# Tiles of B and C from the common ring of a selective scan, and a group of its output matmuls moved by one unit

## Chip, cores and metric

The kernel runs on one core of a Trainium2 chip, in one launch, on an input of 16 samples. The metric is the device time of that core in microseconds (us). The time before is the median of three runs. The profile is one further execution, recorded by the hardware profiler.

## What is computed

Each sample is an image of 256 channels and 32 x 32 positions, so L = 1024 tokens. Two layers are applied, each behind a group normalisation and with a residual sum: an attention layer with four heads and a feed-forward part, and a selective scan (Mamba) with 512 inner channels d and 64 states n. The scan is what matters here:

```
u     = silu(causal_conv(in_proj(x)))              # [L, 512]
dt, Bm, Cm = split(u @ x_proj_w.T, [16, 80])       # Bm, Cm: [L, 64]
delta = softplus(dt @ dt_proj_w.T + dt_proj_b)     # [L, 512]
A     = -exp(A_log)                                # [512, 64]
for t in range(L):
    h = exp(delta[t, :, None] * A) * h + (delta[t] * u[t])[:, None] * Bm[t, None, :]
    y[t] = sum over n of h[:, n] * Cm[t, n]
out   = ((y + u * D) * silu(z)) @ out_proj_w.T * gate
```

## The kernel before, in words

**Units and blocks.** The scan of a sample is cut into 256 units. A unit holds two channels: 64 states of each fill the 128 partitions, and time runs along 1024 columns. Eight units make a block, which fills one of two tiles h0 and h1 in turn (parity e, line 934). The main loop (L1014 to L1055) goes through all 4096 units of the 16 samples; `at` is the unit's place in its sample, i its place in its block.

**A unit's steps.** `load` (L895) fetches a row pair of delta u from DRAM, spread over 64 partitions each, into a tile dub (L913). `inputs` (L916) multiplies it by B on POOL (L918). `decay` (L920) makes delta on PE from three bf16 pieces, by two matmuls into PSUM (L927), and takes exp(delta A) on ACT (L929). `scan` (L931) is one DVE instruction (L935) from those two into h. In iteration n the program writes load(n+6), inputs(n+4), scan(n), decay(n+2), in this order. The exp's PSUM tile has two buffers, so decay(n+2) needs scan(n) to be done.

**Outputs.** `outputs` (L952) makes the sum over n with C, block by block, while the next block is scanned. It is a generator: each iteration of the main loop takes it to its next `yield`, ahead of the scan and of decay(n+2). A block has 16 groups (r, s) of matmuls (L960), which read all of its h tile and a spread form of C, cd. After the four groups of each r ACT copies 256 columns to y2 (L966). Before, a yield stands after every second group, so that in each of the eight units of the next block PE takes two groups. In the ninth unit 32 small matmuls turn the result (L972), ACT copies it to yo (L976), and three units later it is stored (L983). The h tile of a block is written again by the block after the next, whose first scan waits for the last group.

**B and C.** At a sample's first load (L898) the tiles bt and ct are fetched, each row of B and C to two partitions (L903). Before, they come from the pool hst with one buffer each. bt is read by every product of the sample. ct is read on ACT by `spread_c` (L941, L944) at units 7 and 8 of the sample, which fills cd, and by nothing afterwards. At a block's first load the pieces of delta are fetched too (L909). The tiles dub come from the pool dutp with seven buffers.

**Side work.** The next sample's attention and scan inputs (`prepare`, L985) and the previous one's gate and output (`gate_and_store`, L836) are generators as well, whose steps are dealt out between the units at a rate set from the steps' shares (L1029, L1052 to L1055). What remains is done at unit 250 (L1030), where the input of the sample after the next is fetched too.

**Queues.** PE, ACT, DVE and POOL keep the order in which the program is written: L1066 to L1076 chain their instructions. Every DMA is issued from SP. SP's order isn't in that chain; it is fixed when the kernel is built, and a DMA can stand ahead of its place in the program where its tile and its data are there (the last sample's ct is issued at 12036.8 us, its bt at 12147.5). When the kernel runs, SP is one queue in order: a DMA that waits for its tile holds what stands behind it. A pool's tiles with one tag share its buffers: a new tile takes the one that comes free.

## Time and profile before

| | |
|---|---|
| median of 3 runs | 12829.15 us (12777.23 to 12891.25) |
| profiled execution | 12813.5 us |
| its span | 12811.7 us |
| mean granted TensorE clock | 0.796 |
| DVE, POOL, PE, ACT busy | 88%, 78%, 77%, 61% of the span |
| first scan starts, last scan starts | 444.0 us, 12761.2 us |
| scans: number, mean | 4096, 2276 ns |
| products with B: number, mean | 4096, 2417 ns |
| exps: number, mean | 4096, 1090 ns |

The span runs from the first to the last instruction of the program, and the execution's time is taken around it. Times in the timeline count from the span's start. A group of the profile shows line, engine, operation, tiles written and read with their shapes and their number; then its busy time in us and the mean duration in ns; then the engine's idle time just before its instructions, with what ended it. In the list of an instruction's waits the two numbers are the total in us and how often. In the timeline the first number is the start, the second the length of a merged stretch, x the number of instructions in it, and the bracket the idle time before it with what ended it. SPq is SP's queue of DMAs; its busy time is that of issuing, and the data moves afterwards.

### The profile page before, as it was taken

Reading aid. Unit: us, or ns where it says so; the run is one execution under the profiler, and the core shown is the slowest. Engines: PE = TensorE matmul, PEld = TensorE weight load, DVE = VectorE, ACT = ScalarE, POOL = GpSimd, SP = SyncE. Lnnn points to the kernel's source line nnn. Section 1 sums busy time; section 2 is a strip of 40 time slices with the busy share of each in tenths; the row PEclk is TensorE's granted clock in tenths of the full one; section 3 lists DMA queues with packets and bytes.
Section 4 is the critical chain, followed back from the end, with each engine's and each line's share of the span. In section 5 each row is a group of like instructions: output and inputs, shape, how many; then the busy total and the mean of one; then the engine's idle time right before and its main releaser. Section 6 shows DMA issues by size and latency. Waiting matters only on the chain. (4 is left out here: it accounts for less than half of the span.)

```text
span 12811.7 us, 424772 instructions
## 1 busy us (share of the span) xinstructions
PE 9896.8 (77%) x186800; PEld 5493.9 (43%) x186800; DVE 11279.1 (88%) x7480; ACT 7776.4 (61%) x10933; POOL 10022.9 (78%) x4201
## 2 busy tenths in 40 slices
PE   6676977868778687886878778697786877868776
PEld 2344444444444444444444444444444444444444
DVE  2789898898988899898998988999888998989998
ACT  3566665656656566566666656666565665656654
POOL 0587877878788787887878778887787878878798
PEclk7887977879878797887878878797787978868756
DMA  1567666676676766767676676766767667676776
GB/s 49 170 218 236 222 219 223 220 242 214 219 234 219 241 213 218 235 215 243 212 233 230 217 237 212 244 218 215 231 219 240 218 218 237 216 240 211 230 251 229
DMA packets 1038405, 2820.13 MB, mean 220 GB/s; under 512 B 290370, under 2 KB 368451, under 8 KB 1036548
## 3 DMA queue, kind: packets, MB, share of 16 engines
q1 hardware_dynamic: 1036548, 2792.97, 66.0%
q8 instruction: 1459, 23.90, 0.8%
q14 instruction: 398, 3.26, 0.1%
HBM read 2513.82 MB, written 261.62 MB: 217 GB/s over the span
## 5 line engine op out<-in xcount | busy, mean ns | idle before, releaser
L918 POOL TENSOR_TENSOR dub<-dub,bt 128x1024 f32<-128x1024 f32 x4096 | 9797.2, 2417 | 2640.4 <-DMA dub<-dus 2468.9
L935 DVE TENSOR_TENSOR_SCAN h<-a,dub 128x1024 f32<-128x1024 f32 x4096 | 9205.6, 2276 | 799.1 <-ACT a L929 475.0
L929 ACT ACTIVATE a<-a,acol 128x1024 f32<-128x1024 f32 x4096 | 4463.7, 1090 | 2870.7 <-PE a L927 2749.6
L960 PEld LDWEIGHTS yb<-h,cd 128*32 128x32 f32 x131072 | 2503.1, 129 | 2812.0 <-issue 1278.9
L960 PE MATMUL yb<-h,cd 128*32 128x64 f32 x131072 | 3274.4, 253 | 479.5 <-ACT y L966 331.3
L927 PE MATMUL a<-pieces,pick 48*128 48x512 bf16 x8192 | 1910.4, 458 | 2158.6 <-DVE h L935 2047.7
L927 PEld LDWEIGHTS <-pick 48*128 48x128 bf16 x8192 | 569.6, 95 | 2564.1 <-issue 2156.1
L966 ACT COPY y<-yb 128x256 f32<-128x256 f32 x2048 | 762.2, 372 | 721.7 <-PE yb L960 713.4
L499 PE MATMUL av<-pt,vv 128*64 128x512 f32 x2048 | 611.0, 677 | 3.0 <-ACT sums L488 1.6
L519 ACT ACTIVATE pt<-st_ps 128x512 f32<-128x512 f32 x1024 | 552.9, 597 | 89.2 <-PE st_ps L511 88.2
L972 PE MATMUL yb<-turn,y 128*32 128x16 f32 x32768 | 592.1, 214 | 7.1 <-issue 5.9
L511 PE MATMUL st_ps<-sp 33*128 33x512 f32 x2048 | 591.3, 653 | 2.9 <-ACT pt L519 2.9
L972 PEld LDWEIGHTS yb<-turn,y 128*32 128x32 f32 x32768 | 574.1, 159 | 8.3 <-issue 6.8
L440 PE MATMUL s_ps<-kd,q 32*64 32x512 f32 x2044 | 543.5, 618 | 17.1 <-DVE mx L419 9.0
L440 PE MATMUL s_ps<-k,q 32*64 32x512 f32 x2048 | 518.4, 593 | 0.0
L976 ACT COPY yo<-yb 128x128 f32<-128x128 f32 x512 | 135.6, 265 | 598.2 <-PE yb L972 586.1
L696 PE MATMUL g_ps<-w,xp 128*128 128x256 f32 x1464 | 455.2, 450 | 0.0
L419 DVE CUSTOM_DVE_ANT_0 over<-s_ps,over 128x512 f32<-128x512 f32 x512 | 342.9, 671 | 82.3 <-ACT over L445 44.6
L696 PEld LDWEIGHTS g_ps<-w,xp 128*128 128x128 f32 x1464 | 368.1, 326 | 66.5 <-issue 58.8
L445 ACT ACTIVATE over<-s_ps 128x512 f32<-128x512 f32 x511 | 303.3, 594 | 40.0 <-PE s_ps L440 40.0
L872 PE MATMUL m_ps<-w,xs 128*128 128x256 f32 x1024 | 318.3, 461 | 11.5 <-POOL xs L847 11.5
L682 DVE SCALAR_TENSOR_TENSOR u<-up,cwh,u 128x1024 f32<-128x1024 f32 x192 | 281.4, 1466 | 28.0 <-ACT u L674 27.7
(182 smaller groups left out, 7363.9 us busy)
## 6 DMA issues: line engine op xcount, KB each, us to landing
dub<-dus SPq DMA_DIRECT2D x4096, 512.0 KB
dps<-pc SPq DMA_DIRECT2D x384, 128.0 KB
pieces<-dps SPq DMA_DIRECT2D x1024, 48.0 KB
xs<-in_x_dram SPq DMA_DIRECT2D x64, 512.0 KB
xs<-kept SPq DMA_DIRECT2D x64, 512.0 KB
zs<-z SPq DMA_DIRECT2D x64, 512.0 KB
ud<-u SPq DMA_DIRECT2D x64, 512.0 KB
dus<-du SPq DMA_DIRECT2D x64, 512.0 KB
```

Of the source, the lines that this page charges most:

```text
L440: nc.tensor.matmul(s[ts(e, 64)], q4[r, ts(c, 64)], keys[r], start=True, stop=True)
L499: nc.tensor.matmul(av[ts(e, 2 * DH)], vv[j // (NJ // 2)][:, j % (NJ // 2), 2 * pair + e, :], pts[e], start=(j == 0), stop=(j == NJ - 1),)
L511: nc.tensor.matmul(s, ka[r, ts(j, P)], qa[r, hs(hf)], start=True, stop=True)
L519: nc.scalar.activation(pt, s, AF.Exp)
L696: nc.tensor.matmul(ps[:, ts(q, C)], xp[k][:, ds(first + t, P, 4)], wg_s[:, k, t, :], start=(k == 0 and t == 0), stop=False,)
L918: nc.gpsimd.tensor_tensor(v, v, blocks[units[n][0]]["bt"], ALU.mult)
L927: nc.tensor.matmul(a[:, hs(hf)], w, pieces[r], start=True, stop=True)
L929: nc.scalar.activation(a, a, AF.Exp, scale=acol[:, at : at + 1])
L935: nc.vector.tensor_tensor_scan(now["h", e][:, i, :], decays.pop(n), loaded.pop(n), 0.0, ALU.mult, ALU.add)
L960: nc.tensor.matmul(yb[ts(g, 32), ts(s, 64)], cd[:, at // 16, ts(c, 32)], hbuf[:, :, at : at + 8], start=(c == 0), stop=(c == 1),)
L966: nc.scalar.copy(y2[:, r], yb[:, :256])
L972: nc.tensor.matmul(some[ts(r, 32), x], y2[:, r, x:256:8], turn[:, x], start=True, stop=True)
```

## The change

bt and ct now come from the pool dutp, under the tag of the dub tiles, and that pool has nine buffers instead of seven. The pool hst loses the two. The memory taken is the same: 7 + 2 tiles of 4 KB a partition before, nine after. A buffer that bt or ct leaves can be taken by a dub tile and the other way round.

In `outputs` the yield after group (3, 1) goes to after group (3, 2). The seventh unit so takes the groups (3, 0), (3, 1) and (3, 2), and the eighth takes (3, 3) and the copy to y2. The number of yields stays.

```diff
@@ -79,7 +79,7 @@
-    dutp = pool("dutp", 7)
+    dutp = pool("dutp", 9)
@@ -896,8 +896,8 @@
         if (k, q, e, i) == (0, 0, 0, 0):
-            bt = hst.tile([P, L], F32, name="bt", tag="bt")
-            ct = hst.tile([P, L], F32, name="ct", tag="ct")
+            bt = dutp.tile([P, L], F32, name="bt", tag="dub")
+            ct = dutp.tile([P, L], F32, name="ct", tag="dub")
             for v, lo in ((bt, 0), (ct, NS)):
                 src = st["rows"][lo : lo + NS, :]
                 nc.sync.dma_start(v, src.unsqueeze(1).to_broadcast([NS, 2, L]))
@@ -964,7 +964,7 @@
                 if s == 3:
                     nc.scalar.copy(y2[:, r], yb[:, :256])
-                if s % 2 == 1:
+                if s % 2 == 1 and (r, s) != (3, 1) or (r, s) == (3, 2):
                     yield
```

## The prediction

> **What bounds the kernel now.** I read the page first: which engine is full, and which rows fill it.

> ```profile
> span 12811.7 us, 424772 instructions
> PE 9896.8 (77%) x186800; PEld 5493.9 (43%) x186800; DVE 11279.1 (88%) x7480; ACT 7776.4 (61%) x10933; POOL 10022.9 (78%) x4201
> ...
> L918 POOL TENSOR_TENSOR dub<-dub,bt 128x1024 f32<-128x1024 f32 x4096 | 9797.2, 2417 | 2640.4 <-DMA dub<-dus 2468.9
> L935 DVE TENSOR_TENSOR_SCAN h<-a,dub 128x1024 f32<-128x1024 f32 x4096 | 9205.6, 2276 | 799.1 <-ACT a L929 475.0
> ```

> DVE is the fullest: 4096 scans and the side work that stands between them. POOL's 2640 us of idling cost nothing by themselves; what counts is DVE's idle time, of which 799.1 us lie just before a scan. So I asked line 935 what it waits for:

> ```profile
>   ACT a L929: 475.0, 458
>   POOL dub L918: 141.2, 60
>   PE yb L960: 92.1, 84
> ```

> Three inputs can be late: the decay (ACT), the product delta u x B (POOL), and the tile h, which must be free of the outputs' matmuls (PE). These labels name the semaphore that moved last, so I checked them against the rows: for each of the 813 waits over 0.06 us I compared the scan's start with the end of its own exp, of its own product and, at the first unit of a block, of the last matmul that reads the old h. Whichever of the three ended last (within 0.6 us of the scan) counts as the cause. Counted so, exps end about 550 us of waits, h's release 153 us (147 waits, all at a block's first unit), and products only 93 us in 18 waits. 15 of these 18, with 92.0 us, are the first unit of samples 1 to 15, 3.2 to 8.2 us each, 6.1 on average. Everywhere else the product is ready long before, a median of 12 us.

> So I opened the timeline there, at the start of sample 6. SP's queue, POOL, DVE:

> ```profile
> 5101.19 8.03 SPq L913 DMA_DIRECT2D dub<-dus  x5
> 5109.27 1.06 SPq L344 DMA_DIRECT2D xs<-in_x_dram  x2
> 5120.88 0.53 SPq L903 DMA_DIRECT2D bt<-rows  x1
> 5121.52 1.00 SPq L909 DMA_DIRECT2D pieces<-dps  x2
> 5122.60 1.17 SPq L913 DMA_DIRECT2D dub<-dus  x2
> ```
> ```profile
> 5109.28 11.58 POOL L918 TENSOR_TENSOR dub<-dub,bt 128x1024 f32<-128x1024 f32 x5 [6.65 <-DMA dub<-dus]
> 5128.63 32.36 POOL L918 TENSOR_TENSOR dub<-dub,bt 128x1024 f32<-128x1024 f32 x14 [7.78 <-DMA dub<-dus]
> ```
> ```profile
> 5111.43 13.19 DVE L935 TENSOR_TENSOR_SCAN h<-a,dub 128x1024 f32<-128x1024 f32 x6 [0.57 <-ACT a L929]
> 5131.02 4.59 DVE L935 TENSOR_TENSOR_SCAN h<-a,dub 128x1024 f32<-128x1024 f32 x2 [6.39 <-POOL dub L918]
> ```

> B has one buffer. Its load stands in SP's queue until POOL's last product of the old sample ends (5120.86), and behind it wait the pieces of delta and the first delta u tiles. The DMA engines fall idle meanwhile (share 0.00 from 5118 to 5122), and DVE then stands 6.39 us. The waits of SP's own queue confirm both halves:

> ```profile
> SPq L913 <- DVE h L935: 6102.8, 3284, 7.0
> SPq L903 <- POOL dub L918: 151.7, 15, 11.5
> ```

> B's load waits at 15 starts, 10 us each. Delta u's loads wait nearly always for a scan: in the rows, load k is issued 0.03 us after scan k-7 ends, the seventh tile back. The ring is full, but it is a cushion: see the 12 us.

> [...] The scan reads a from PSUM and dub from SBUF; products take 2327 at least and 2355 ns in the median, so shifting products against scans should change no duration.

> **The change, part by part.** No operation is added or removed; the number of loads, products, scans and matmuls stays.

> (1) B and C in the common ring, at a sample's start. In mid-sample B holds one of nine, leaving eight. Loads take slots in order, so delta u's 255 goes after scan 247, then B after scan 248, C after 249, unit 256 after scan 250. In the shown start scans 245 to 249 end by 5110.9 and scan 250 by 5113.6. So B is issued near 5109 instead of 5120.88, and unit 256's load near 5113.6 instead of 5122.60. From issue to product half of all loads take 4.9 to 7.1 us; C and B together add 2 x 512 KB, at the 300 GB/s of that stretch 2 x 1.7 us. Landing lies between 5113.6+5.6=5119.2 and 5113.6+7.1+3.4=5124.1. POOL is free at 5120.9, a product takes 2.34: ready between 5123.2 and 5126.4. Scan 255 ends at 5124.6. What is left of the stall is 0 to 1.9 us; I take 0.9. Saved: 15 x (6.1-0.9) = **79 us**, between 15 x (6.1-1.9) = 63 and all 92. What is late next is the exp of unit 256: it also waited, since its pieces stood behind B (PE line 927 idles 59 us on pieces, 15 times), and comes forward with them. C's load is moved too, past the pieces and delta u's loads into a busier stretch; its reader, line 944, comes seven units later.

> (2) The eighth slot in mid-sample. The cover is already a median of 12 us, and outside sample starts products cost DVE 1.2 us: **0**, bounds 0 and -1. For the first eight units C still holds a slot, so there are seven as before, six for the first two; the working above includes that.

> (3) The moved group: 16 loads and 16 matmuls, 0.25 us at full clock and 0.43 at half (two groups fill 0.65 and 1.08). It is taken from behind the seventh unit's decay to before it. PE keeps program order, so h is released earlier only where PE idles between; the same group makes the seventh unit's decay, hence the exp for the next block's first unit, later where PE has no idle time before it. Both occur:

> ```profile
> 666.09 0.65 PE L960 MATMUL yb<-h,cd 128*32 128x64 f32 x32
> ```
> ```profile
> 1111.39 0.61 PE L927 MATMUL a<-pieces,pick 48*128 48x512 bf16 x2 [1.75 <-DVE h L935]
> ...
> 1113.98 1.08 PE L960 MATMUL yb<-h,cd 128*32 128x64 f32 x32
> ```
> ```profile
> 1115.23 2.29 DVE L935 TENSOR_TENSOR_SCAN h<-a,dub 128x1024 f32<-128x1024 f32 x1 [0.51 <-PE yb L960]
> ```

> At 666 us PE runs without a break from the seventh unit's groups through the decay and attention's matmuls to the eighth's: moving a group changes no end. At 1111 PE stands 1.75 us for a scan before the decay; there the group fits and h comes 0.43 earlier, against a wait of 0.51. Going through all blocks with the least of group, idle time and wait gives a gain of at most 18 us (53 blocks); the delay of exps that have less than the shift to spare gives a loss of at most 16 us (67 blocks), part of it won back where PE sets the pace. I take **-5 us**, bounds -18 and +16.

> Sum: 79+0+5 = 84 us off the profiled execution, 12813.5 (span 12811.7 and 1.8 around it), is 12729.5. The median of the runs is 15.65 higher, 12829.15, so I predict **12745 us** (-0.65%).

> **Rivals.** (A) Much more is won: h's release leaves the path altogether, because the schedule shifts as well. 92+153 = 245 us: 12584. For it: these waits exist and the group aims at them. Against: in 94 of the 147 PE has no gap for the group. Half way, 12660. Chance 0.18 for below -1%.
> (B) The start's stall is only replaced: unit 256's load takes its slot late, because SP holds it for the old B tile (free only at 5120.86, as now) or for scan 251. Then load and product come some 2 to 3 us earlier than now, not 9: 15 x 2.5 = 38, plus 5: about 12787. If the tile's order undoes even that, the change does nothing: 12829. Together 0.25.
> (C) Slower: the exp of each block's first unit falls on the path, at the seventh unit's decay. Price 0.25 to 0.43 us x 511 blocks = 128 to 220 us, against 79 saved. With the mean of the two prices, 0.34, it decides against the change once 79/0.34 = 230 blocks have less spare than the group, and over 1% slower takes (79+128)/0.43 = 480 blocks at the dearer one; 67 have less now. 12829+220-79 = 12970 at worst. Chance 0.07.
> The forecast itself, between -1% and about -0.4%: 0.50.

> **How the numbers follow.** 1% is about what a measurement of this kernel can tell from no change; the three runs alone spread from 12777 to 12891. Faster by over 1%: 0.20 (A and a tail of the forecast); slower: 0.07 (C); same: 0.73. The range reaches half way into A and past no change for the scatter of a median: 12640 to 12840. The forecast's own range, from its bounds (92+1+18 and 63-16): 12718 to 12782.

> **What would show it.** Right: the 15 gaps at sample starts fall from 6.1 to under 2 us, the B load no longer waits for POOL, products lose nothing elsewhere, and scans' waits for exps stay near 475 with h's release lower by at most 18. Loads issued at the end of scan k-8 show the eighth slot. Wrong: starts with a new wait of 3 us and more (pieces, exps, product 256), or exps' waits at first units up by over 50 us, or a changed total without a change in these.

## The result, and the profile after

| | before | after |
|---|---|---|
| median, 20 runs each | 12824.53 us (12774.17 to 12893.92) | 12823.81 us (12680.96 to 13016.91) |
| ratio, 95% interval | 1 | 0.9975 (0.9951 to 0.9999) |
| profiled execution | 12813.5 us | 12719.86 us |
| its span, mean granted clock | 12811.7 us, 0.796 | 12718.0 us, 0.799 |

The gain is 0.25%, about 32 us, where 84 us (0.65%) were forecast. Ratios in this document leave out executions more than 1.5% above a kernel's fastest (3 of the changed kernel's 20, 11 of 16 of the ring of nine alone below), while medians and ranges take all runs, so for a kernel whose times spread wide the ratio is kinder than the median.

The two rows of numbers contradict each other: the profiled execution fell by 94 us, a little more than forecast, and the median by nothing. A single profile of the changed kernel, read alone, would have confirmed the forecast. Its page, first part and the two main groups:

```profile
span 12718.0 us, 424804 instructions
PE 9905.2 (78%) x186800; PEld 5500.1 (43%) x186800; DVE 11335.2 (89%) x7480; ACT 7773.6 (61%) x10933; POOL 9987.3 (79%) x4201
...
L918 POOL TENSOR_TENSOR dub<-dub,bt 128x1024 f32<-128x1024 f32 x4096 | 9761.9, 2411 | 2593.2 <-DMA dub<-dus 2424.0
L935 DVE TENSOR_TENSOR_SCAN h<-a,dub 128x1024 f32<-128x1024 f32 x4096 | 9203.4, 2276 | 711.1 <-ACT a L929 500.9
```

Idle time before scans fell from 799.1 to 711.1 us. But DVE's busy time, with the same 7480 instructions, rose from 11279.1 to 11335.2: 56 us, though no instruction was added. The scans are not it (9205.6 to 9203.4). What the scans wait for, line 935:

```profile
  ACT a L929: 500.9, 496
  PE yb L960: 117.1, 83
  POOL dub L918: 56.5, 53
```

Sorted by which input ended last, as in the prediction, products now end 4.8 us of waits instead of 93, all at sample starts and none over 1.1 us; h's release 134 instead of 153; exps 570 instead of about 550. 3141 of the 4096 loads of delta u now go out within 0.2 us of the end of scan k-8; before, 3537 went out so after scan k-7. With the eighth slot in use a product is done 12.4 us ahead of its scan in the median instead of 10.1. The start of sample 5 in the timeline, SP's queue, then POOL, then DVE:

```profile
4284.85 0.52 SPq L903 DMA_DIRECT2D bt<-rows  x1
4287.03 0.52 SPq L903 DMA_DIRECT2D ct<-rows  x1
4287.64 1.12 SPq L909 DMA_DIRECT2D pieces<-dps  x2
4289.36 2.87 SPq L913 DMA_DIRECT2D dub<-dus  x2
```
```profile
4298.48 9.31 POOL L918 TENSOR_TENSOR dub<-dub,bt 128x1024 f32<-128x1024 f32 x4 [2.62 <-DMA dub<-dus]
```
```profile
4300.85 4.63 DVE L935 TENSOR_TENSOR_SCAN h<-a,dub 128x1024 f32<-128x1024 f32 x2 [0.62 <-POOL dub L918]
```

B's load goes out at 4284.85, while POOL still multiplies the old sample (until 4295.86: the next product starts at 4298.48, after 2.62 us of idling), and the scan stands 0.62 us where at the start shown before it stood 6.39. In SP's queue the 151.7 us of the loads of line 903 waiting for POOL are gone; they now wait for scans, 28.4 us in all. The removed wait is really removed. Two questions are left: where DVE's 56 us come from, and why the median does not follow the profile.

**The clock.** The second has a first answer in the runs themselves. Over the changed kernel's 20 runs time and mean granted clock lie on a line: correlation -0.987, 13.3 us more for each 0.001 of clock less; 59 runs of the kernel before give 12.95 us per 0.001 (-0.97). Lined up at one clock, 0.790, the changed kernel takes 12834 us and the kernel before 12883 to 12906, depending on the session: 49 to 72 us apart. So the changed kernel gets a lower clock in many runs (0.776 to 0.802, 0.7913 on average, where the 59 of the kernel before have 0.780 to 0.801 and 0.7932), and its time follows. The distance between the two lines isn't the gain by itself, though: experiment 1 shows such a distance for a kernel whose ratio shows no gain. The clock records of either profile hold two values, 0.5 and 1.0 (314 stretches of each in that of the kernel before); the mean counts how long it is 0.5. The experiments ask which part does that, and where.

### The profile page after: what moved, and what is told of

Same layout as the page of the kernel before. It is cut to its first block, busy times and chain, and to the rows that moved or that the text cites. A ratio compares the mean times of both kernels' runs of the same rounds, so it can differ in the third digit from the quotient of the medians.

```text
span 12718.0 us, 424804 instructions
## 1 busy us (share of the span) xinstructions
PE 9905.2 (78%) x186800; PEld 5500.1 (43%) x186800; DVE 11335.2 (89%) x7480; ACT 7773.6 (61%) x10933; POOL 9987.3 (79%) x4201
## 4 chain that ended last, share of the span: by engine, by line
PE 40%; DVE 29%; issue 11%; ACT 11%; DMA 6%; POOL 3%; SPq 1%; DVEq 0%; POOLq 0%; ACTq 0%
DVE h L935 22%; PE yb L960 7%; PE s_ps L440 7%; PE a L927 6%; ACT a L929 5%; DMA dub<-dus 3%; PE av L499 3%; PE st_ps L511 3%; POOL dub L918 2%; PE yb L972 2%; PE z_ps L647 2%; PE g_ps L696 1%; PE m_ps L872 1%; PE qk_ps L404 1%; DVE u L682 1%
## 5 line engine op out<-in xcount | busy, mean ns | idle before, releaser
L918 POOL TENSOR_TENSOR dub<-dub,bt 128x1024 f32<-128x1024 f32 x4096 | 9761.9, 2411 | 2593.2 <-DMA dub<-dus 2424.0
L935 DVE TENSOR_TENSOR_SCAN h<-a,dub 128x1024 f32<-128x1024 f32 x4096 | 9203.4, 2276 | 711.1 <-ACT a L929 500.9
L929 ACT ACTIVATE a<-a,acol 128x1024 f32<-128x1024 f32 x4096 | 4465.0, 1090 | 2821.1 <-PE a L927 2756.2
L960 PEld LDWEIGHTS yb<-h,cd 128*32 128x32 f32 x131072 | 2506.5, 129 | 2829.3 <-issue 1295.8
L960 PE MATMUL yb<-h,cd 128*32 128x64 f32 x131072 | 3279.1, 253 | 487.6 <-ACT y L966 339.9
L927 PE MATMUL a<-pieces,pick 48*128 48x512 bf16 x8192 | 1911.4, 458 | 2076.1 <-DVE h L935 2026.3
L927 PEld LDWEIGHTS <-pick 48*128 48x128 bf16 x8192 | 572.3, 95 | 2479.2 <-issue 2112.2
```

The costliest lines, as they stand in the source:

```text
L918: nc.gpsimd.tensor_tensor(v, v, blocks[units[n][0]]["bt"], ALU.mult)
L927: nc.tensor.matmul(a[:, hs(hf)], w, pieces[r], start=True, stop=True)
L929: nc.scalar.activation(a, a, AF.Exp, scale=acol[:, at : at + 1])
L935: nc.vector.tensor_tensor_scan(now["h", e][:, i, :], decays.pop(n), loaded.pop(n), 0.0, ALU.mult, ALU.add)
L960: nc.tensor.matmul(yb[ts(g, 32), ts(s, 64)], cd[:, at // 16, ts(c, 32)], hbuf[:, :, at : at + 8], start=(c == 0), stop=(c == 1),)
```

## Experiments

**1. Which part: the ring alone, the group alone, nothing, a smaller ring.** The first four ran on one chip.

```diff
# ring alone (nine); ring of eight: the same with 8
-    dutp = pool("dutp", 7)
+    dutp = pool("dutp", 9)
-            bt = hst.tile([P, L], F32, name="bt", tag="bt")
-            ct = hst.tile([P, L], F32, name="ct", tag="ct")
+            bt = dutp.tile([P, L], F32, name="bt", tag="dub")
+            ct = dutp.tile([P, L], F32, name="ct", tag="dub")
# group alone
-                if s % 2 == 1:
+                if s % 2 == 1 and (r, s) != (3, 1) or (r, s) == (3, 2):
```

The ring of nine alone:

> Only B and C in the common ring of nine; the output groups stay two and two. Theory 1 (the moved group eats the gain[...]): ratio 0.993 to 0.994, as forecast, and the waits at sample starts 5 us in place of 92. Theory 2 (the eighth slot eats it: POOL runs elsewhere against DVE's side work and the DVE operations with two SBUF operands, lines 682 and 725, get some 60 us longer together): ratio 0.997 to 0.998 as for the whole change, line 725 near 2380 ns a piece. Theory 3 (neither part: the gain is there at a given granted clock, and the clock differs from run to run): time falls on one line with the granted clock, some 12 us for 0.001, 60 to 90 us under that of the kernel before.

The group alone:

> Only the moved group. Theory 1: slower, ratio 1.003 to 1.005, with a granted clock 0.003 to 0.005 lower in the mean. Theory 2: 0.999 to 1.001, and line 725 near 1757 ns. Theory 3: 0.999 to 1.001, on the clock line of the kernel before. The wait for h's release at first units of blocks falls by at most 18 us.

The kernel before, unchanged, as a measure of the method:

> The kernel before, unchanged, to have the granted clock beside the time of each of its runs. All theories: ratio 1.000 within 0.002. Theory 3 asks for a slope of some 12 us for 0.001 of clock, as in the runs of the changed kernel; theories 1 and 2 have no need of one, but theory 1 asks for a mean clock above that of the changed kernel's runs (0.791).

A ring of eight, which keeps the start's gain but gives delta u's tiles only seven slots in mid-sample, as before:

> B and C in the common ring, but of eight: seven slots for delta u in mid-sample as before, six for the first eight units, and B is still fetched ahead of the old sample's end. Groups two and two. Theory 2: the sample starts keep most of the gain (waits of 92 us fall to 5 to 30) and lines 682 and 725 stay as before, so ratio 0.993 to 0.996, better than with nine. Theories 1 and 3: as e1_ring or up to 30 us slower.

| | median | ratio, 95% | mean clock of the runs | product waits at starts |
|---|---|---|---|---|
| ring of nine | 13003.98 | 1.0003 (0.9960 to 1.0046) | 0.7803 | 3.9 us |
| group | 12782.44 | 0.9984 (0.9959 to 1.0009) | 0.7930 | 88.5 us |
| before again | 12805.99 | 0.9970 (0.9937 to 1.0004) | 0.7946 | 94.3 us |
| ring of eight | 12774.25 | 0.9952 (0.9929 to 0.9974) | 0.7955 | 16.6 us |

The kernel before, measured against itself, comes out at 0.9970; so one ratio near 0.9975, the changed kernel's included, says little. The moved group isn't what ate the gain: alone it does nothing that can be told from the kernel before again. The ring of nine removes the waits at the starts and is no faster for it, with a median 148 us above that of the kernel before in its session (12855.58), at by far the lowest clock. The ring of eight keeps most of the gain and its clock. What sets the two rings apart is the eighth slot in mid-sample, which the prediction had put at 0.

At clock 0.790 the ring of nine stands at 12852 us, the ring of eight at 12847 and the kernel before at 12896. But the group alone stands there too, at 12842, with the waits at the starts untouched (88.5 us) and a ratio that shows no gain (its interval allows for 0.4%). Either the group gains more than the 18 us that were forecast for it at most, or the distance of two lines isn't what a change is worth; no run settles that. The lines show where the spread comes from.

Of the three theories, the first is out: the group alone isn't slower. The second foretold the ring of eight, but not that the ring of nine would do worse than the whole change. The third has its line, but what the distance is worth is open. In the ring of nine the group isn't neutral either: with it (the changed kernel) the median is 12823.81, without it 13003.98, in different sessions. Why is open.

**2. Where the clock falls.** In the profile of the ring of nine (span 12979.4 us) samples 2, 5, 6 and 9 took 839 to 858 us between their first scans and the next sample's, the others about 775. Inside these samples one stage of the side work is the cause, the matmuls of line 440, which make the next sample's attention scores for their maxima: 32 x 64 tiles of the array, eight in each unit, over 32 units. Here is its entry in an ordinary sample (1327) and in sample 2 (2105), PE:

```profile
1327.18 0.39 PE L927 MATMUL a<-pieces,pick 48*128 48x512 bf16 x2
1328.08 1.07 PE L440 MATMUL s_ps<-kd,q 32*64 32x512 f32 x4 [0.51 <-DVE kd L414]
...
1330.85 1.07 PE L440 MATMUL s_ps<-kd,q 32*64 32x512 f32 x4
...
2104.80 0.39 PE L927 MATMUL a<-pieces,pick 48*128 48x512 bf16 x2
2106.49 1.07 PE L440 MATMUL s_ps<-kd,q 32*64 32x512 f32 x4 [1.31 <-DVE kd L414]
...
2110.11 1.97 PE L440 MATMUL s_ps<-kd,q 32*64 32x512 f32 x4
```

PE waits for kd, a subtraction on DVE, 0.51 us in the one case and 1.31 in the other. One unit later the same four matmuls take 1.07 and 1.97 us. Why kd is late, DVE and then POOL at both places:

```profile
1327.34 0.69 DVE L414 TENSOR_TENSOR kd<-k 128x512 f32<-128x512 f32 x1 [2.05 <-ACT k L407]
...
2104.94 1.50 DVE L414 TENSOR_TENSOR kd<-k 128x512 f32<-128x512 f32 x1 [2.22 <-ACT k L407]
```
```profile
1327.66 4.87 POOL L918 TENSOR_TENSOR dub<-dub,bt 128x1024 f32<-128x1024 f32 x2 [4.04 <-DMA dub<-dus]
...
2103.54 5.10 POOL L918 TENSOR_TENSOR dub<-dub,bt 128x1024 f32<-128x1024 f32 x2 [3.19 <-DMA dub<-dus]
```

The subtraction takes 0.69 us where it starts ahead of POOL's product, and 1.50 where POOL is already in one; the pairs of products take 4.87 and 5.10 us where two mostly take 4.7. And this is what the late entry costs: 24 us of the stage at either place (columns: stretch, its length, busy us and number of PE, weight loads, DVE, ACT, POOL, granted clock, DMA share, GB/s):

```profile
1327.00:1351.00 24.00, 23.49 (x422) 9.68 (x410) 22.99 (x24) 14.65 (x22) 18.52 (x8) 1.00 0.73 223
2130.00:2154.00 24.00, 24.00 (x250) 8.53 (x244) 14.00 (x15) 8.84 (x12) 10.29 (x5) 0.50 0.28 98
```

PE is busy for 23.49 and 24.00 us, but at clock 0.50 it gets 250 matmuls done instead of 422, and DVE, otherwise full, stands for 10 of 24 us. A unit takes 5.16 us instead of 2.79 in the median, and the clock stays at 0.50 for 160 us, to the end of the stage: 164 to 167 us instead of 91.6, **75 us a sample**. All 16 entries of the stage in this profile: the four that fell had PE idle for 1.24 to 2.17 us (kd 1423 to 2350 ns); of the twelve others ten were at 1.04 us and less, one is the program's first, ahead of all scans (1.42), and one came through at 1.30. In the profile of the kernel before kd takes 0.66 to 0.69 us in 14 of 16; of the two late ones (1090 and 1110 ns) one cost 34 us at half clock; in that of the ring of eight the one late kd (1642 ns, PE idle 1.46) is the one stage that fell. In the changed kernel's profile nine kd take 0.79 to 1.25 us and no stage fell: it is a run without a loss. That the changed kernel loses stages in other runs is inferred, from their clocks and from what experiment 3 does to them. One such stage would explain the slope too. It adds 165 us at half clock, which lowers a run's mean by about 0.5 x 165/12800 = 0.0064, and 75 us: 11.7 us per 0.001, where the runs of the kernels so far show 11.7 to 14.3. The changed kernel's slowest run is 336 us above its fastest, which would be four to five such stages; timed runs have no trace in which to count them.

**3. Take the lateness away.** The scan has one operand in PSUM and one in SBUF, and POOL's products don't show in its length: in the profile of the kernel before the 1915 scans that products overlap from end to end take 2276 ns on average, the 192 that none overlaps 2275. If the late kd is the cause, the same form might free it; that was the author's estimate. One half of k stands in PSUM when line 414 runs, so line 414 can read it there. It then no longer needs ACT's copy of that half; everything else stays.

```diff
-        nc.vector.tensor_tensor(kd, k4[:, hs(0)], k4[:, hs(1)], ALU.subtract)
+        nc.vector.tensor_tensor(kd, k4[:, hs(0)], ps, ALU.subtract)
```

In the changed kernel, in the ring of nine alone (two expectations, as it ran twice) and in the kernel before:

> The whole change, and line 414 takes the second half of k from its PSUM tile instead of SBUF: the same numbers, but one SBUF operand in place of two, and no wait for ACT's copy. Theory A (the eighth slot shifts POOL's products onto line 414; PE then stands over 1.2 us ahead of the first matmul of line 440, the TensorE clock falls to half there and stays so through the whole stage, 75 us a sample): no sample of the profile has the stage of line 440 at half clock, the mean granted clock is 0.798 or more in nearly all runs, the median 12690 to 12730, ratio 0.988 to 0.992, and the runs spread by less than 60 us. Rival B ([...]line 414's length is a by-product): median 12800 to 12830 and a spread of 200 us and more as for the changed kernel.

> Only the ring of nine, with line 414 from PSUM. Theory A: from 13004 down to 12700 to 12750, no stage at half clock. Rival B: 12950 to 13050 as e1_ring.

> The fastest version so far once more, for a firmer number: ring of nine, groups two and two, line 414 from PSUM. Theory A: again no stage of line 440 at half clock, 12700 to 12750, ratio 0.990 to 0.995. If e6_ring_kd was a lucky draw, 12800 and more in part of the runs.

> The kernel before with line 414 from PSUM. Theory A: the runs that lost a stage to half clock come back, so median 12760 to 12790 (ratio 0.994 to 0.997) with a spread under 60 us; the changed kernel treated likewise (e5_after_kd) is then 60 to 90 us faster than this one, which is the forecast gain. Rival B: 12800 to 12860 with the spread of the kernel before.

| line 414 from PSUM in | median | range | ratio to before, 95% |
|---|---|---|---|
| before | 12778.99 | 12745 to 12801 | 0.9981 (0.9967 to 0.9995) |
| changed kernel | 12728.04 | 12703 to 12752 | 0.9938 (0.9919 to 0.9957) |
| ring of nine | 12709.90 | 12665 to 12729 | 0.9921 (0.9900 to 0.9941) |
| ring of nine, second time | 12696.82 | 12686 to 12727 | 0.9883 (0.9836 to 0.9931) |

The group of line 414 in the changed kernel so edited:

```profile
L414 DVE TENSOR_TENSOR kd<-k,qk_ps 128x512 f32<-128x512 f32 x16 | 11.0, 686 | 41.5 <-ACT k L407 41.5
```

686 ns on average where the changed kernel has 846; five of the 16 lie wholly inside a product and take 688 ns. An earlier start isn't what helped: DVE idles 41.5 us ahead of these 16, and 41.4 in the changed kernel. No stage falls to half clock in any of these profiles, and the changed kernel's spread shrinks from 336 us over 20 runs to 49 over six. The late kd is the cause of the lost stages. Not all of the expectations came: the changed kernel's ratio was to be 0.988 to 0.992 and its clock 0.798 in nearly all runs (0.796 to 0.801, two of six at 0.798 or more), and it was to be 60 to 90 us faster than the kernel before so treated (it was 51). The ring of nine with this edit has the lowest medians, without the moved group; its intervals overlap with the changed kernel's.

**4. The reverse: make kd late in the kernel before.** The subtraction is made three times, so that two of the three are repeated work.

```diff
         nc.vector.tensor_tensor(kd, k4[:, hs(0)], k4[:, hs(1)], ALU.subtract)
+        for _ in range(2):
+            nc.vector.tensor_tensor(kd, k4[:, hs(0)], k4[:, hs(1)], ALU.subtract)
```

> The kernel before, with the subtraction of line 414 made three times, so that PE stands 1.4 us longer ahead of line 440 once in a sample, with nothing else moved. Theory A: most of the 15 samples run the stage at half clock, 10 to 15 of them at 75 us each, so 13500 to 13900. Rival B: 15 x 1.4 = 21 us slower, about 12850 to 12880.

Median 13352.81 us, ratio 1.0427 (1.0406 to 1.0449), mean clock 0.764. The two extra subtractions take 44.5 us in all; the time rose by 554 over the before of its session. PE was idle 1.6 to 4.5 us before the stage, mostly 3.98, because the extra subtractions took 1.39 us each on average and not 0.69; so the pause was longer than meant and longer than in the ring. Every stage after the first sample's lost 17 to 122 us at half clock and 7 to 55 us of time, 490 us together. So the mechanism works in a kernel that has no part of the change. The size was missed (13500 to 13900 expected): these stages recovered before their end, those of the ring did not. What decides that is open.

**5. PE's idle time, or kd's length?** The ring of nine with line 414 as it was, and one more matmul on PE between kd and its readers, of ready data, whose output nothing reads:

```diff
+        nc.tensor.matmul(
+            psum("fill_ps"), wqk_s[:, 0, ts(1, P)], xn[0][:, hs(1)], start=True, stop=True
+        )
```

> The ring of nine with line 414 as before, from SBUF and blocked by POOL at times; but one more matmul of 128 x 512 (0.99 us of work on PE that nothing reads) stands between the last matmul of line 404 and line 414's readers, in the time in which PE waits. Theory A (PE's idle time ahead of line 440 makes the clock fall): line 414 is still 0.8 to 2.3 us in most samples, yet hardly a stage runs at half clock; median 12700 to 12760 instead of 13004. Rival C (it is line 414's length itself, by what it delays behind it): 12950 to 13050 as e1_ring.

Median 12746.36 us (12696 to 12811), ratio 0.9948 (0.9925 to 0.9971), mean clock 0.7983 against 0.7803 of the ring without the fill. kd is as slow as in the ring:

```profile
L414 DVE TENSOR_TENSOR kd<-k 128x512 f32<-128x512 f32 x16 | 16.6, 1040 | 41.3 <-ACT k L407 41.3
```

Two of them took 1497 and 2006 ns, and PE's idle time before the stage was 0.26 and 0.77 us there and none at the other 14. No stage lost its clock. So it is PE's pause that counts, and the late kd because it makes one. The runs still spread over 115 us, and their clocks from 0.794 to 0.802; whether a stage fell in some of them isn't known.

**6. Two more, with line 414 from PSUM: the ring of eight and the group alone.**

> B and C in the common ring of eight (seven slots for delta u in mid-sample, as before), groups two and two, line 414 from PSUM. Theory A: nothing is shifted in mid-sample, so lines 682 and 725 stay at some 282 and 112 us where nine slots cost 47 us more; sample starts keep 10 to 20 us of their wait. Against e7_before_kd 70 us less: 12690 to 12730, the same as nine slots or up to 30 us better. Rival B (the eighth slot gives as much as it takes): 12740 and more.

> Only the moved group, line 414 from PSUM, so that no stage falls to half clock by it. As predicted for that part: 5 us under e7_before_kd, bounds 18 less and 16 more, so 12760 to 12795 and a ratio of 0.997 to 0.999. If the group took part in the loss, 20 us and more above e7_before_kd.

The ring of eight: 12745.57 us, ratio 0.9952 (0.9932 to 0.9971). The expectation was missed, and the number is the rival's: with line 414 mended, eight buffers are no better than nine (12709.90 and 12696.82). So the eighth slot seems to give back what it takes from DVE, once the clock is out of the way; the next section says where. Its line 725 stays short (112.0 us) but line 682 lengthens to 298.5, which the theory of the eighth slot doesn't explain; it stays open. The group: 12783.63 us, ratio 0.9976 (0.9958 to 0.9994), beside 12778.99 for the kernel before with the same edit on another chip. It does nothing that shows, as forecast.

## Why the prediction was wrong

**Step 1, B and C in the ring: right.** Forecast 79 us, bounds 63 to 92; the waits at the 15 starts went from 92.0 to 4.8 us, 87 saved. C's moved load cost nothing that shows.

**Step 3, the moved group: right in size.** Forecast -5, bounds -18 and +16. h's release gave 19 us back, and the waits for exps at blocks' first units rose by 13 (81 to 95 us). Alone its ratio is 0.9984, its interval on both sides of 1: nothing that shows.

**Step 2, the eighth slot: this failed.** The prediction gave it 0, bounds 0 and -1, because no scan waits for a mid-sample product, "a median of 12 us". (The 12 us count from the product's start; from its end it is 10.1. It makes no difference here.) That cover answers only whether a product comes too late. It doesn't answer what else a product meets when it comes at another time. The step rested on the sentence "shifting products against scans should change no duration", an estimate from the least and the median time of a product (2327 and 2355 ns). It holds for the scan, one operand of which is in PSUM: 2276 ns before and after, and with or without a product beside it (experiment 3). But DVE has other instructions between the scans, and seven lines of the side work read two operands from SBUF (414, 555, 579, 624, 682, 725, 843). The prediction didn't go through them, and the least and the median don't show what happens there: in the profile of the kernel before the 3556 products that overlap none of the seven lines take 2327 to 2480 ns, the other 540 up to 3452. The lines themselves, where no product overlaps them, take at most 0.69 us (the tiles of 512 columns) and 1.29 us (those of 1024); with a product beside them up to 2.41 and 3.45. For line 414 0.69 us becomes 1.50 in the lines above, 2.35 at most, and with one operand in PSUM it was never over 0.69 in six profiles. Three things followed.

- DVE's own time. The two lines that grew most, in the kernel before and then in the changed one:

```profile
L682 DVE SCALAR_TENSOR_TENSOR u<-up,cwh,u 128x1024 f32<-128x1024 f32 x192 | 281.4, 1466 | 28.0 <-ACT u L674 27.7
L725 DVE SCALAR_TENSOR_TENSOR u<-up,u 128x1024 f32<-128x1024 f32 x64 | 112.5, 1757 | 18.6 <-ACT up L720 18.6
```
```profile
L682 DVE SCALAR_TENSOR_TENSOR u<-up,cwh,u 128x1024 f32<-128x1024 f32 x192 | 305.2, 1590 | 28.0 <-ACT u L674 27.7
L725 DVE SCALAR_TENSOR_TENSOR u<-up,u 128x1024 f32<-128x1024 f32 x64 | 152.4, 2381 | 18.6 <-ACT up L720 18.6
```

 Together 63.7 us longer; line 555 is 9.3 us shorter. The seven lines together grow by 58 us, which is all of DVE's 56. An instance of the two that no product overlaps takes 1.2 to 1.3 us, the longest 3.4; length and overlap with POOL go together in each line (correlation 0.73 and 0.89 in the changed kernel's profile), in part because a longer instance overlaps more. That their lengthening comes from POOL is read off this and the case of line 414; no run took it away for these two lines.

- Less waiting in DVE's side work, which the prediction didn't have either. Lines 843 and 555 wait for DMAs, and with the eighth slot they wait less. All profiles but experiment 4's, sums in us:

| | seven slots in mid-sample (7 profiles) | eight slots (6 profiles) |
|---|---|---|
| line 682 busy | 280 to 288, once 298.5 | 300 to 315 |
| line 725 busy | 105 to 113 | 122 to 152 |
| DVE idle before line 843 | 117 to 143 | 87 to 104 |
| DVE idle before line 555 | 23.5 to 28 | 9 to 12 |

 The rings of eight and of nine with line 414 mended differ in this slot alone, so these waits go with it; why the DMAs come earlier no run asks. Between the kernel before and the changed kernel with line 414 from PSUM, where no stage of line 440 falls, lines 682 and 725 grew by 46.9 us and these two waits fell by 34.2. So for these two parts 0 was nearly right as a sum, but by luck: the step named neither.

- The clock. Line 414 is such an instruction too, and PE waits for it just ahead of the stage of line 440. This is what the step cost. The change is worth 0.0043 or 55 us where line 414 is mended (0.9981 to 0.9938; the medians say 51). In the changed kernel mending it gains 0.0037 or 47 us (0.9975 to 0.9938), in the kernel before 0.0019 or 24. So some 23 us more are lost to the clock than before, and 32 are left. That is one way to write four measured ratios, not a check of them; each is good to 0.002 or so, 25 us, and they come from several sessions. Of the other 29 us between the 84 forecast and 55, the first two points account for 13; the rest is within what the ratios can tell.

**From the profile to the median: this failed too.** The prediction took the median as the profile plus a constant 15.65 us. The distance isn't a constant: the median is 9 us below the profile for the kernel before with mended line 414 (12778.99 and a profile of 12787.83), 104 above it for the changed kernel. By experiments 2 and 3 much of it should be the stages that fell in a run, whose number changes from run to run; timed runs don't show them.

**The rivals.** A (much more is won) is refuted: h's release hardly moved. B (the stall is only replaced) comes near in its number but not in its place: the stall is gone. C, the exps of the first units, cost 13 us instead of 128 and more. None of them had the clock, nor the side work on DVE. Among the signs that would show it right, the start gaps under 2 us, the B load that no longer waits for POOL and the loads at the end of scan k-8 all came; of those that would show it wrong, "a changed total without a change in these". The account of the starts was true, and it wasn't the whole.

## What to carry to other kernels

A wait that goes away moves other engines in time, so before a shift is priced at nothing, go through every instruction that the moved work may now meet, not only the one that it feeds: here POOL's products moved, and they met seven lines on DVE with two operands in SBUF, one of which went from 0.69 us to 2.35 at most and stayed at 0.69 with one operand in PSUM. Ask also what the delayed instruction feeds: PE's pause of 1.31 us in place of 0.51 ahead of a stage of small matmuls cost 75 us in a sample of the ring of nine, and with one ready matmul in the pause no stage of the profile fell. And when runs spread, plot time against mean granted clock before a median or a single profile is believed: it says where the spread comes from. It doesn't replace an experiment on the gain: at equal clock the moved group alone looked 54 us faster, where its ratio shows no gain.
